# A decoder layer in float32: the second layer's v turned by VectorE and gathered through memory, or by TensorE head by head

## The chip, the cores and the metric

The kernel runs on one core of one Trainium2 chip. The metric is device time in microseconds, the median of several executions. A core has five engines that run side by side, each in the order of its own instructions: TensorE (PE in the profile, PEld for its weight loads), VectorE (DVE), ScalarE (ACT), GpSimd (POOL) and SyncE (SP), which here issues all DMAs. TensorE writes to PSUM, a small memory in banks; DMAs move data between HBM and SBUF.

## The reference, cut to what matters

Three layers follow each other, each with a residual and a layer norm. x has 16 sequences of 256 tokens with 512 channels.

```
x = layernorm(x + mamba_like(x, ...))            # first layer: projections, a causal
                                                 # convolution, a scan, gates
x = layernorm(x + xattn(x, k, bias, ctx, ctx))   # second layer
x = layernorm(x + ffn(x, ...))                   # third: W x + b, and the two best of 8 LoRA experts

# second layer, 32 heads of 8 tokens each; L = 512 channels
kv = v[b,h,i,:] * ctx[b,h,j,:]                   # outer product over i, j = 8 x 8
y  = causal_convolution(kv, k[h], along the 512) + kv * bias[h,i]
out[b,h,j,:] = sum over i of y[b,h,i,j,:] * ctx[b,h,i,:]
```

v is the output of the first layer. Its convolution along the channels is a product with a Toeplitz matrix, so v is wanted with channels on partitions, while the first layer delivers it with tokens on partitions.

## The kernel before

The program is written with a manual schedule: each engine runs its instructions in the order in which the code issues them, and only semaphores for data hold them back.

**First half** (to about 750 us). Eight groups of 512 tokens, four tiles `xs[t]` of 128 tokens x 512 channels each. The loop over `order` has ten steps `i`, each a pair of projections. At the end of a group the output products are added onto `xs`, and `normalised` (L542 to L549) takes the statistics (`layer_norm_stats`: DVE, then a power on POOL), scales the tile on DVE (L547) and stores it to the DRAM tensors `first[0]` and `first[1]` (L549, rows of 2 KB): tiles 0 and 2 at the end of the group, tiles 1 and 3 (`late`) in steps 0 and 1 of the next. Step 1 also issues the loads of the next group's x. The last group does all four tiles in the order 0, 2, 1, 3; between them it loads head 0's v.

**Second half.** A loop over the heads `h`, 0 to 31. For each, `load_v` (L140) fetches 128 rows (16 sequences x 8 tokens) of 512 channels, and `turned_v` (L147, L149) turns them with four transposes of TensorE into the PSUM tile `tr`, which ACT copies to the SBUF tile `vT`. DVE's `products` (L157) multiply `tr` with the context `cT` into `kv`; POOL adds `vT` as the residual. The rows are turned at the turn of the heads, one head before they are used.

The convolution of a head goes in two halves `q`, each into two PSUM tiles `y0` and `y1` of two banks, which exist once. So the order around the turn of a head is: the last convolution (q = 1, quadrant matmuls L1046) ends; DVE multiplies `y1`, then `y0` with `cT` (`multiplied`, L1079) and reduces them (L1089); meanwhile TensorE does `turned_v`, the transpose of the gates (`turned_gates`: L1244, ACT's copy L1246), a share of the feed-forward; then `seeded` (L1013) writes the first product of the new head to a bank of `y1`, ACT copies it to the other bank of `y1` (`spread_seed`, L1020), TensorE does another share of the feed-forward, and `convolve` goes on with its full products (L1031): the first to `y0`, the second to a bank of `y1`.

The feed-forward of two heads is one `Pair` of seven half products. From head 4 on, an even head finds the pair `opened` (its products `sixth` and `second` are due), an odd head from 5 on finds it `closing` (`seventh` and `lora_of_second`). The two lines that follow the seed in `spread_seed` are

```
for a, b in ((0, HP), (HP, 0)):
    nc.scalar.copy(bank_of(y, 2)[b : b + HP], seed[a : a + HP])
```

SP's queue in a head is: the Toeplitz tile of the next head (`load_T`, which waits for the convolution to be through), v and context of the head after next, and outputs of 256 KB.

Of the kernel before, what the change touches and what calls it, by code (L numbers as in the profile page):

```python
# [8 lines left out]
F32 = mybir.dt.float32  # L9
# [5 lines left out]
P = 128  # L15
# [15 lines left out]
NL = D // P  # L31
NE, R = 8, 16
HP = P // 2

# [36 lines left out]
def decoder_kernel(  # L73
# [34 lines left out]

    dram = ctx.enter_context(tc.tile_pool(name="dram", bufs=1, space=bass.MemoryType.DRAM))
    SH = S // P  # L110
    first = [dram.tile([B, P, D], F32, name=f"first{i}") for i in range(SH)]
    wp = ctx.enter_context(tc.tile_pool(name="w", bufs=1))

    big = ctx.enter_context(tc.tile_pool(name="big", bufs=2))
# [19 lines left out]
        nc.sync.dma_start(cT, ctxT[h])  # L134
        return cT

    def load_v(h):
        vn = q3.tile([P, D], F32, tag="vn", name="vn", bufs=1)
        sh, hs = divmod(h, P // NH)
        nc.sync.dma_start(vn, first[sh][:, hs * NH : (hs + 1) * NH, :])  # L140
        return vn

    def turned_v(vn, pool, tag):

        tr = pool.tile([P, NQ, NL, BQ * NH], F32, tag=tag, name="tr")
        for k, blk in enumerate(BLOCKS_IN):
            nc.tensor.transpose(tr[:, :, k, :], vn[:, blk * P : (blk + 1) * P], ident)  # L147
        vT = q2.tile([P, NQ, NL, BQ * NH], F32, tag="vT", name="vT")
        kept = nc.scalar.copy(vT, tr)  # L149
        return vT, tr, kept  # L150

    def products(vT, cT, kv, q, ks=(0, NL // 2), kept=None):

        full = [P, NL * BQ // 2, NH, NH]
        for k in ks:
            blks = slice(k, k + NL // 2)
            last = nc.vector.tensor_tensor(  # L157
                kv[:, q, k * BQ : (k + NL // 2) * BQ],
                vT[:, q, blks].rearrange("p k (b i) -> p (k b) i", i=NH).unsqueeze(2)
                .to_broadcast(full),  # L160
                cT[:, q, 1 + k : 1 + k + NL // 2].rearrange("p k (b j) -> p (k b) j", j=NH).unsqueeze(3)
                .to_broadcast(full),
                ALU.mult,
            )
            if kept is not None:
                wait_for(last, kept)
        return last

    def wait_for(ins, other):
# [12 lines left out]
    with ExitStack() as s1:  # L182
# [357 lines left out]
                part = w[:, kc, 0:cols]  # L540
                nc.vector.tensor_tensor(part, part, ps[:, 0:cols], ALU.subtract)

        def normalised(g, *ts):

            stats = [layer_norm_stats(nc, p2, nhalf, r, "a") for _, r in ts]
            for (t, r), (mv, rs) in zip(ts, stats):
                nc.vector.tensor_scalar(r, r, mv[:, 0:1], rs, ALU.subtract, ALU.mult)  # L547
                bi, sh = divmod(g * TT + t, SH)
                nc.sync.dma_start(first[sh][bi], r)  # L549

        heads = {}
        late, sums = [], []
        for g in range(groups):
            xs = xs_next
            more = g + 1 < groups
# [95 lines left out]
            for i, (kind, p) in enumerate(order):  # L651
# [71 lines left out]
                        w_sums = w_o_sums(behind)  # L723
                        next(w_sums)
                before = (kind, p, al, be, u, to)
                if i < 2 and late:
                    normalised(g - 1, late.pop(0))
                if i == 1 and more:
                    xs_next = load_x(g + 1)

            def spread_heads(cc):
# [94 lines left out]
            if more:  # L826
# [23 lines left out]
                for n, (al, be) in enumerate(banks):  # L850
                    out_product(al[:, 0:S], n, (0, 1), (1, 0), upon=True)
                    if n == 0:
                        next(parts)
                    out_product(be[:, 0:S], n, "S4", (1, 1), upon=True)
                    if n == 0:
                        next(parts)
                    out_product(be[:, S:], n, (1, 1), "T4", upon=True)
                    out_end_sums(n, al, be, us[n])
                    if n == 0:
                        next(parts)  # L860
                        next(parts)
                        normalised(g, (0, xs[0]), (2, xs[2]))
                late = [(1, xs[1]), (3, xs[3])]
            else:
                finish_sums()
                gated(1, spread_heads(1))
                for n, t in enumerate((0, 2, 1, 3)):


                    ps = ps_s.tile([P, 512], F32, tag="s", name="s") if n in (0, 3) else bank()  # L870
                    for c in range(NI):
                        for j in range(2):
                            nc.tensor.matmul(  # L873
                                ps[:, j * S : (j + 1) * S],
                                zs[c][:, t * P : (t + 1) * P],
                                w_o[c // HC, j][c % HC],
                                start=(c == 0 and j == 0),
                                stop=(c == NI - 1),
                                skip_group_check=True,
                            )  # L880
                        if n == 3 and c == 3:
                            heads["vT"] = turned_v(heads["vn"].pop(0), ps_t, "tr")
                            heads["vn"] = [load_v(1)]
                    if n == 3:
                        for q in range(NQ):
                            products(heads["vT"][0], cTs[0], kvs[0][0], q)
                    r = xs[t]
                    nc.vector.scalar_tensor_tensor(r, r, 2.0, ps, ALU.mult, ALU.add)
                    normalised(g, (t, r))
                    if n == 1:  # L890
                        heads["vn"] = [load_v(0)]
                        kvs = [load_T(0), load_T(1)]
            if g == 0:
                skip_bc = wp.tile([P, S], F32, name="skip_bc")
                nc.sync.dma_start(skip_bc, skip.partition_broadcast(P))
# [21 lines left out]
    with ExitStack() as s2:  # L917
# [267 lines left out]

        w_lb = w2.tile([ER, D], F32, name="w_lb")
        nc.sync.dma_start(w_lb, loraB)
        vT_next, vns = heads["vT"][0], heads["vn"]
        more_next = prepared(*kvs[0])
        sk_next = skip_sums(0, kvs[0][0])  # L1190
        more_next[2](1)
# [1 line left out]
        vT_ahead = []  # L1193

        def ahead():
            vT_ahead.append(turned_v(vns.pop(0), ps_t, "tr"))
            vns.append(load_v(2))
            cTs.append(load_c(2))

        def squares(o_l):  # L1200
# [72 lines left out]
                )[n - 1]  # L1273
                nc.gpsimd.tensor_tensor(Tw[:, n - 1], one, other, ALU.subtract)

        def half_product(ps, a, w, start=False):
            for kc in range(2):
                nc.tensor.matmul(  # L1278
                    ps, a[:, kc, :], w[:, kc, :], start=(start and kc == 0), stop=(kc == 1),
                    skip_group_check=True,  # L1280
                )

        class Pair:
# [36 lines left out]
            def sixth(self):  # L1320
                half_product(self.al[:, HI], self.S[2], Tw[:, 1])

            def second(self):
                half_product(self.al[:, LO], self.half(0, 1), corner(1, 0))

            def common(self):
                u, m = self.u, p2.tile([P, HD], F32, tag="m", name="m", bufs=1)
# [28 lines left out]
                    skip_group_check=True,  # L1356
                )

            def lora_of_second(self):
                nc.tensor.matmul(  # L1360
                    self.be[:, HI], self.xaT[1], w_lb[:, LO], start=False, stop=True,
                    skip_group_check=True,
                )
                lora(self.al, self.xaT[1], HI, True)

            def parts(self, head):
                if head == 0:
# [3 lines left out]
            def finish(self, head):  # L1371
                return Finish(self.f + head, self.parts(head), self.rs[head])

        last, xa = None, None
        pair, closing, ready = None, None, []
        for h in range(HX):
            nxt, ff, f = h + 1 < HX, last is not None, h - 1
# [7 lines left out]
            y = new_y()  # L1385
            if h:
                if nxt:
                    v_after = turned_v(vns.pop(0), ps_t, "tr")
                    kvs.append(load_T(h + 1))
                    if h + 2 < HX:  # L1390
                        vns.append(load_v(h + 2))
                        cTs.append(load_c(h + 2))
                if xa is not None:
                    xaT = turned_gates(xa, gl[:, XAT])
                    if h == 2:
                        xaT_alone = xaT
                    else:
                        pair.xaT.append(xaT)
                opened = pair if pair is not None and len(pair.o) == 2 else None
                if h == 2:  # L1400
                    feed_forward(base, alone, (1,))
                if h == 3:
                    lora(base, xaT_alone, ALL)
                if opened is not None:
                    opened.sixth()
                if closing is not None:
                    closing.seventh()
                seed = seeded(y, T, xs, 0, h == 1)
                spread_seed(y, seed, h == 1)
                if h == 2:  # L1410
                    feed_forward(base, alone, (2,))
                if opened is not None:
                    opened.second()
                if closing is not None:
                    closing.lora_of_second()
            if h < 2:
                weight_differences((3, 1) if h == 0 else (2, 4))
            if ff:
# [40 lines left out]
            behind = None  # L1459
            if nxt:  # L1460
                kv_n, T_n = kvs[0]
                cT_n, (vT_next, v_n, kept) = cTs[0], v_after
                if h:
                    behind = products(v_n, cT_n, kv_n, 0, kept=kept)

            if h:
                contract(y, cT, red, 0, (1, 0))
            else:

                prs = []  # L1470
                products(v_n, cT_n, kv_n, 0, (0,), kept)
                prs = [multiplied(y, cT, 0, i) for i in (1, 0)]
                behind = products(v_n, cT_n, kv_n, 0, (NL // 2,), kept)
                for i, pr in zip((1, 0), prs):
                    reduced(pr, red, 0, i)
            y = new_y()
# [223 lines left out]
```

## Time and profile before

| | |
|---|---|
| median of 3 runs | 1408.8 us (1408.38 to 1408.83) |
| the profiled execution | 1408.37 us, its span 1406.6 us |
| TensorE busy, weight loads | 1391.9 us, 946.6 us |
| VectorE busy | 1182.1 us |
| ScalarE, GpSimd busy | 427.5 us, 613.3 us |
| DMA, HBM read and written | 63 GB/s over the span, 70.62 and 17.32 MB |

The span goes from the first to the last instruction; the execution's time has some 1.8 us around it. The rows of a timeline are: start, duration, engine, line of the code, operation, tiles written and read, shapes, number of instructions merged, and in brackets how long the engine stood before it and what released it. A float32 matmul is recorded as two passes. "PEld" rows are weight loads; one that waits for a semaphore holds back its matmul.

### The profile page before, as it was taken

Reading aid. Unit: us, or ns where it says so; the run is one execution under the profiler, and the core shown is the slowest. Engines: PE = TensorE matmul, PEld = TensorE weight load, DVE = VectorE, ACT = ScalarE, POOL = GpSimd, SP = SyncE. Lnnn points to the kernel's source line nnn. Section 1 sums busy time; section 2 is a strip of 40 time slices with the busy share of each in tenths; the row PEclk is TensorE's granted clock in tenths of the full one; section 3 lists DMA queues with packets and bytes.
Section 4 is the critical chain, followed back from the end, with each engine's and each line's share of the span. In section 5 each row is a group of like instructions: output and inputs, shape, how many; then the busy total and the mean of one; then the engine's idle time right before and its main releaser. Section 6 shows DMA issues by size and latency. Waiting matters only on the chain.

```text
span 1406.6 us, 19577 instructions
## 1 busy us (share of the span) xinstructions
PE 1391.9 (99%) x7091; PEld 946.6 (67%) x7091; DVE 1182.1 (84%) x2269; ACT 427.5 (30%) x948; POOL 613.3 (44%) x818
## 2 busy tenths in 40 slices
PE   9999999999999999999999999999999999999997
PEld 7888888788888888878885445455545454555444
DVE  6988878878888787877867888989898898989886
ACT  2423323233232333332311223333332333333222
POOL 5450011110100201001004667887777877887774
PEclk9999999999999999999999999999999999999999
DMA  8114121120121111202103122211222122212100
GB/s 305 33 38 134 27 67 46 38 85 8 40 83 46 47 45 39 85 10 70 66 8 104 43 68 75 76 56 65 61 75 69 52 75 76 75 46 75 61 27 38
DMA packets 49169, 89.21 MB, mean 63 GB/s; under 512 B 8880, under 2 KB 13360, under 8 KB 49072
## 3 DMA queue, kind: packets, MB, share of 16 engines
q1 hardware_dynamic: 49072, 87.96, 19.7%
q8 instruction: 56, 0.92, 0.3%
q14 instruction: 41, 0.34, 0.1%
HBM read 70.62 MB, written 17.32 MB: 63 GB/s over the span
## 4 chain that ended last, share of the span: by engine, by line
PE 96%; DVE 2%; issue 1%; DMA 0%; POOL 0%; ACT 0%; SPq 0%; POOLq 0%; DVEq 0%
PE mm L330 21%; PE y L1031 15%; PE s L330 14%; PE y L1046 12%; PE s L782 6%; PE mm L782 6%; PE y L1013 4%; PE be L1278 4%; PE al L1278 3%; PE gl L1223 2%; PE tr L147 1%; PE xm L599 1%; PE mm L739 1%; PE mm L873 1%; PE al L1250 1%; PE s L873 1%
## 5 line engine op out<-in xcount | busy, mean ns | idle before, releaser
L1079 DVE TENSOR_TENSOR pr<-y,cT 128x1024 f32<-128x1024 f32 x126 | 148.5, 1220 | 50.2 <-PE y L1046 50.2
L1046 PE MATMUL y<-kv 64*64 64x512 f32 x1536 | 179.6, 598 | 0.0
L588 DVE SCALAR_TENSOR_TENSOR acc<-xi,wc,acc 128x512 f32<-128x512 f32 x192 | 141.9, 753 | 7.4 <-ACT acc L584 1.8
L1089 DVE TENSOR_REDUCE red<-pr 128x128 f32<-128x1024 f32 x126 | 147.1, 1210 | 0.0
L157 DVE TENSOR_TENSOR kv<-tr,cT 128x1024 f32<-128x1024 f32 x124 | 145.6, 1216 | 0.0
L1046 PEld LDWEIGHTS y<-kv 64*64 64x64 f32 x1536 | 52.2, 132 | 118.6 <-issue 97.1
L1031 PE MATMUL y<-kv 128*128 128x512 f32 x272 | 128.5, 594 | 1.9 <-DVE pr L1079 1.7
L68 POOL TENSOR_TENSOR rs_a<-ve_a,nhalf 128x1 f32<-128x1 f32 x32 | 18.9, 592 | 242.3 <-DVE ve_a L66 242.3
L391 POOL TENSOR_TENSOR rstd<-ms,nhalf 128x4 f32<-128x4 f32 (+1 forms) x9 | 8.5, 949 | 251.3 <-DVE ms L389 251.3
L1031 PE MATMUL y<-kv,Td 128*128 128x512 f32 x248 | 116.5, 592 | 0.0
L330 PE MATMUL mm<-XT,w_z 128*128 128x256 f32 x384 | 90.7, 379 | 0.0
L1031 PEld LDWEIGHTS y<-kv,Td 128*128 128x128 f32 x248 | 47.1, 190 | 59.3 <-issue 59.1
L1020 ACT COPY y<-y 64x512 f32<-64x512 f32 x120 | 67.0, 558 | 59.3 <-PE y L1013 57.4
L997 POOL TENSOR_TENSOR xs<-kv 128x512 f32<-128x512 f32 x63 | 80.4, 1277 | 0.1
L1031 PEld LDWEIGHTS y<-kv 128*128 128x128 f32 x272 | 50.9, 189 | 42.8 <-ACT y L1020 17.9
L330 PEld LDWEIGHTS mm<-XT,w_z 128*128 128x128 f32 x384 | 73.0, 190 | 9.9
L1428 POOL TENSOR_TENSOR ol<-o,red 128x512 f32<-128x512 f32 x31 | 39.3, 1268 | 73.1 <-DVE red L1089 73.1
L330 PE MATMUL mm<-xnT,w_z 128*128 128x256 f32 x288 | 70.7, 382 | 0.0
L223 POOL TENSOR_TENSOR XT<-xnT 128x512 f32<-128x512 f32 x7 | 9.2, 1318 | 129.0 <-PE mm L782 129.0
L1013 PE MATMUL y<-xs,kv 128*128 128x512 f32 x120 | 62.6, 604 | 0.5 <-issue 0.2
L330 PE MATMUL s<-XT,w_xi 128*128 128x256 f32 x256 | 61.0, 380 | 0.8 <-DVE XT L226 0.5
L330 PEld LDWEIGHTS mm<-xnT,w_z 128*128 128x128 f32 x288 | 54.0, 190 | 10.1 <-issue 3.0
(333 smaller groups left out, 3058.8 us busy)
## 6 DMA issues: line engine op xcount, KB each, us to landing
cT<-in_ctxT SPq DMA_DIRECT2D x32, 384.0 KB
kv<-in_toep SPq DMA_DIRECT2D x32, 384.0 KB
xt<-in_x SPq DMA_DIRECT2D x32, 256.0 KB
spread<-both SPq DMA_DIRECT2D x32, 256.0 KB
first<-xt SPq DMA_DIRECT2D x32, 256.0 KB
vn<-first SPq DMA_DIRECT2D x32, 256.0 KB
out<-res SPq DMA_DIRECT2D x31, 256.0 KB
xnT<-in_xT SPq DMA_DIRECT2D x7, 1024.0 KB
```

Source lines behind the costliest of these rows:

```text
L157: last = nc.vector.tensor_tensor(kv[:, q, k * BQ : (k + NL // 2) * BQ], vT[:, q, blks].rearrange("p k (b i) -> p (k b) i", i=NH).unsqueeze ...
L330: nc.tensor.matmul(ps, w[:, p, a, kc, :], Xs[b][:, kc, :], start=start and kc == 0, stop=stop and kc == 1, skip_group_check=upon,)
L588: ins = nc.vector.scalar_tensor_tensor(acc, xi[:, :, k : k + S], wc[:, c, k : k + 1], acc, ALU.mult, ALU.add)
L782: nc.tensor.matmul(ps, own[a][c][:, n * P : (n + 1) * P], w_o[b][c], start=start and c == 0, stop=stop and c == HC - 1, skip_group_check=upon,
L997: return nc.gpsimd.tensor_tensor(xs[:, q], moving(kv, q, 0), moving(kv, q, 1), ALU.add)
L1013: nc.tensor.matmul(seed, T[:, SHARED_AT, :], xs[:, q], start=True, stop=True)
L1020: nc.scalar.copy(bank_of(y, 2)[b : b + HP], seed[a : a + HP])
L1031: nc.tensor.matmul(bank_of(y, lb), w, moving(kv, q, mb), start=not late and lb not in begun, stop=False, skip_group_check=True,)
L1046: return nc.tensor.matmul(bank_of(y, lb)[cols], T[rows, DIAGONAL_AT, (b - a) * HP : (b - a + 1) * HP], moving(kv, q, lb)[rows], start=star ...
L1079: nc.vector.tensor_tensor(pr.rearrange("p (k b j) i -> p k b j i", k=2, j=NH), y[i].rearrange("p k (b j i) -> p k b j i", j=NH, i=NH), cT[ ...
L1089: nc.vector.tensor_reduce(red[:, q, 2 * i : 2 * i + 2, :].rearrange("p k t -> p (k t)"), pr, AX.X, ALU.add)
L1278: nc.tensor.matmul(ps, a[:, kc, :], w[:, kc, :], start=(start and kc == 0), stop=(kc == 1), skip_group_check=True,)
```

## The change

It has four parts. In the first half, ACT scales the normalised tile, with a factor and an offset that POOL makes ready; the tile's scaling stands a step or more behind its statistics. DVE then turns it in blocks of 32 x 32 in place, and four DMAs a tile store it in pieces of 32 tokens (128 bytes) to `first`, whose layout is now channel first. The first eight tokens of each sequence also go to `rows`, unturned, for head 0, which TensorE still turns. The channels of a row are interleaved (`order_in`), so that a partition of the turned v gathers its pieces.

In the second half, `load_vT` gathers a head's v, already turned, in pieces of 8 tokens (32 bytes), two heads ahead; ACT copies it from SBUF to the PSUM tile `tr` (`kept_in`), where `products` reads it as before. And the small work around the seed is laid anew: half of `second` and half of `lora_of_second` go in front of the seed, and in an even head from 4 on the transpose of the gates goes behind it. The load of the next group's x goes from step 1 to step 3 in all groups but the first.

```
-    first = [dram.tile([B, P, D], F32, name=f"first{i}") for i in range(SH)]
+    first = [dram.tile([P // TB, P, NL, B, TB], F32, name=f"first{i}") for i in range(SH)]
+    rows = dram.tile([B, NH, D], F32, name="rows")
...
+    def load_vT(h, pool, bufs):
+        vT = pool.tile([P, NL, NQ, BQ * NH], F32, tag="vT", name="vT", bufs=bufs)
         sh, hs = divmod(h, P // NH)
-        nc.sync.dma_start(vn, first[sh][:, hs * NH : (hs + 1) * NH, :])
+        tb, part = divmod(hs, TB // NH)
+        nc.sync.dma_start(
+            vT.rearrange("p k q (b i) -> p (k q b) i", i=NH),
+            first[sh][tb].rearrange("p k b t -> p (k b) t")[:, :, part * NH : (part + 1) * NH],
+        )
+        return vT.rearrange("p k q t -> p q k t")
+
+    def kept_in(vT, pool, tag):
         tr = pool.tile([P, NQ, NL, BQ * NH], F32, tag=tag, name="tr")
-        for k, blk in enumerate(BLOCKS_IN):
-            nc.tensor.transpose(tr[:, :, k, :], vn[:, blk * P : (blk + 1) * P], ident)
-        vT = q2.tile([P, NQ, NL, BQ * NH], F32, tag="vT", name="vT")
-        kept = nc.scalar.copy(vT, tr)
-        return vT, tr, kept
+        nc.scalar.copy(tr, vT)
+        return tr
...
-        def normalised(g, *ts):
-            stats = [layer_norm_stats(nc, p2, nhalf, r, "a") for _, r in ts]
-            for (t, r), (mv, rs) in zip(ts, stats):
-                nc.vector.tensor_scalar(r, r, mv[:, 0:1], rs, ALU.subtract, ALU.mult)
-                bi, sh = divmod(g * TT + t, SH)
-                nc.sync.dma_start(first[sh][bi], r)
+        def spreads_of(r):
+            mv, rs = layer_norm_stats(nc, p2, nhalf, r, "a")
+            nb = p2.tile([P, 1], F32, tag="nb_a", name="nb_a")
+            nc.gpsimd.tensor_scalar(nb, mv[:, 0:1], rs, -1.0, ALU.mult, ALU.mult)
+            return nb, rs
+        def normalised(g, t, r, stats):
+            nb, rs = stats
+            nc.scalar.activation(r, r, AF.Identity, bias=nb, scale=rs)
+            bi, sh = divmod(g * TT + t, SH)
+            if sh == 0:
+                nc.sync.dma_start(rows[bi], r[0:NH])
+        def turned(g, t, r):
+            nc.vector.transpose(r, r)
+            bi, sh = divmod(g * TT + t, SH)
+            for tb in range(P // TB):
+                nc.sync.dma_start(
+                    first[sh][tb].rearrange("(n l) k b t -> (l k) n b t", l=TB // NL)[:, :, bi],
+                    r[tb * TB : (tb + 1) * TB].rearrange("l (n t) -> l n t", t=TB),
+                )
...
-                if i < 2 and late:
-                    normalised(g - 1, late.pop(0))
-                if i == 1 and more:
+                if g:
+                    for one in turning[:2]:
+                        turned(g - 1, *one)
+                    del turning[:2]
+                    if i < 2:
+                        t, r, *_ = late[i]
+                        late[i] = t, r, spreads_of(r)
+                    if i in (1, 2):
+                        normalised(g - 1, *late[i - 1])
+                        turning.append(late[i - 1][:2])
+                if i == (3 if g else 1) and more:
                     xs_next = load_x(g + 1)
...
                     if n == 1:
-                        heads["vn"] = [load_v(0)]
+                        heads["vn"] = load_rows()
                         kvs = [load_T(0), load_T(1)]
+                        for n_, t_ in enumerate((0, 2)):
+                            turned(g, t_, xs[t_])
+                        heads["next"] = load_vT(1, q2, 2)
+                turned(g, 1, xs[1])
+                turned(g, 3, xs[3])
...
         def ahead():
-            vT_ahead.append(turned_v(vns.pop(0), ps_t, "tr"))
-            vns.append(load_v(2))
+            vT_ahead.append(kept_in(vTs[0], ps_t, "tr"))
+            vTs.append(load_vT(2, p2, 3))
             cTs.append(load_c(2))
...
                 if nxt:
-                    v_after = turned_v(vns.pop(0), ps_t, "tr")
+                    v_after = kept_in(vTs[0], ps_t, "tr")
                     kvs.append(load_T(h + 1))
                     if h + 2 < HX:
-                        vns.append(load_v(h + 2))
+                        vTs.append(load_vT(h + 2, p2, 3))
                         cTs.append(load_c(h + 2))
...
+                if opened is None:
+                    turn_gates()
...
                 if opened is not None:
                     opened.sixth()
+                    opened.second((0,))
                 if closing is not None:
                     closing.seventh()
+                    closing.lora_of_second((0,))
                 seed = seeded(y, T, xs, 0, h == 1)
+                if opened is not None:
+                    turn_gates()
                 spread_seed(y, seed, h == 1)
...
                 if opened is not None:
-                    opened.second()
+                    opened.second((1,))
                 if closing is not None:
-                    closing.lora_of_second()
+                    closing.lora_of_second((1,))
```

## The prediction

> **What bounds the kernel now.** I read the page first, then the group of line 147 (the transposes to be removed), then the timeline of single heads, engine by engine, then the DMA view. The page's engine row, its chain and its DMA queue:
>
> ```profile
> PE 1391.9 (99%) x7091; PEld 946.6 (67%) x7091; DVE 1182.1 (84%) x2269; ACT 427.5 (30%) x948; POOL 613.3 (44%) x818
> PE 96%; DVE 2%; issue 1%; DMA 0%; POOL 0%; ACT 0%; SPq 0%; POOLq 0%; DVEq 0%
> q1 hardware_dynamic: 49072, 87.96, 19.7%
> ```
>
> TensorE carries the chain, and DMA is a fifth full. The removed work, from the view of line 147:
>
> ```profile
> L147 PE MATMUL tr<-ident,vn x128: 272/273/330, 749.5 to 1344.9; 128*128 128x128 f32 x128
> ```
>
> Now the turn of one head (an even one), in the timelines of PE, PEld, DVE and ACT:
>
> ```profile
> 907.20 0.66 PE L147 MATMUL tr<-ident,vn 128*128 128x128 f32 x4
> 907.69 0.27 PE L1244 MATMUL gl<-ident,xa 128*128 128x128 f32 x1
> 907.80 1.03 PE L1278 MATMUL al<-Tw,S 128*128 128x256 f32 x4
> 908.66 1.06 PE L1013 MATMUL y<-xs,kv 128*128 128x512 f32 x2
> 909.56 1.03 PE L1278 MATMUL al<-w_f,ol 128*128 128x256 f32 x4
> 910.42 1.45 PE L1031 MATMUL y<-kv 128*128 128x512 f32 x3
> ...
> 908.59 0.30 PEld L1013 LDWEIGHTS y<-xs,kv 128*128 128x128 f32 x2 [0.17 <-issue]
> 910.96 0.51 PEld L1031 LDWEIGHTS y<-kv 128*128 128x128 f32 x2 [0.34 <-ACT y L1020]
> ...
> 907.30 2.36 DVE L1079 TENSOR_TENSOR pr<-y,cT 128x1024 f32<-128x1024 f32 x2 [1.34 <-PE y L1046]
> ...
> 909.76 1.15 ACT L1020 COPY y<-y 64x512 f32<-64x512 f32 x2 [1.06 <-PE y L1013]
> ```
>
> Call 907.20, when the last head's convolution is through, C. The reader is to see two waits that the transposes only just cover. First, the seed matmul (L1013) writes a bank that the first DVE multiplication (L1079, 1.22 us each) must have read: that ends at C+1.33, and the seed's weights load at C+1.40, held back 0.17. Second, ACT copies the seed to another bank from C+2.56 to C+3.71, and the convolution's second full product, which writes those banks, loads its weights at C+3.76, held by that copy. Its matmul starts at 910.42+2x0.43 = C+4.08. So after the second wait TensorE has only about 0.2 us in hand.
>
> **The change part by part.**
>
> *Transposes off TensorE (gain, mostly not kept).* Between the starts of 907.20 and 907.69 four transposes take 0.49 us. They stand at the turn of heads 1 to 30, 30x0.49 = 14.7 us, and once more inside head 0, where DVE is late anyway (TensorE waits 1.0 and 0.7 us for L1079 there). The Trainium skill, "TensorE: Matmul & The Clock Gate", Part 4, has about 275 ns for one transpose in a kernel; that would make 33 us. The trace has the same 273 ns as duration, but the starts lie 0.11 apart, since they are pipelined: I use 0.49 a head. Taken out, TensorE reaches the seed earlier, and the first wait stops it: DVE still ends at C+1.33, weights at C+1.40. The change puts in front of the seed 1.29 us of work in an even head (four matmuls of 0.86, two of 0.43) and 1.40 in an odd one (0.11+0.86+0.43): TensorE idles there where it transposed. Behind the seed 0.43 us of work went forward, so the gain can only appear there, and the second wait allows C+3.76 plus some 0.11 for the loading weights (what the seed shows: its two passes stand 0.47 instead of 0.43 apart): C+3.87 for C+4.08, 0.21 a head. Odd heads 5 to 31 have it: 14x0.21 = 2.9 us.
>
> *The gates' transpose moved (loss).* In even heads from 4 on, the transpose of the gates and ACT's copy of it (L1246, 0.27 us) now stand between the seed and ACT's two copies. ACT is in order: the transpose starts at 909.56, ends 0.27 later, so ACT's copies start at 910.04 to 910.17 instead of 909.76 (a copy's next neighbour starts between 0.17 and 0.30 later). That is 0.28 to 0.41 late against 0.21 in hand: 0.07 to 0.20 lost, 14 heads, 1.0 to 2.8 us; I take 1.9. Behind ACT wait the second full product and all of the convolution. Heads 0 to 3 are bound by DVE or ACT in the same places: 0.
>
> *Copy kept.* ACT's copy of v (586 ns, L149) stays, now from SBUF to PSUM, and no longer waits for TensorE: it runs in ACT's idle time before C (ACT idles 2.14 us before it now). DVE reads the same PSUM tile, six microseconds later. 0; if v were late, ACT would stand with the seed's copies queued behind it, and each microsecond would be one of the kernel.
>
> *Gather.* A head's v came as 128 rows of 2 KB; it now comes as 8192 pieces of 32 bytes. Two rows bound the price of a piece. The window of the store of `row` (512 pieces of 4 bytes) has 528 packets in 0.6 us at 41.8% of 16 engines: 7.6 ns each. The page's 49,072 packets of 1.8 KB took 19.7% of 16x1406.6: 90 ns each. A straight line gives 9 ns for 32 bytes and 13 for 128. So 512 pieces on each of 16 engines: 4.6 us; at the dear end 46 us. A rule speaks against the change: the Trainium skill, "VectorE: DVE Perf Modes", The three transpose paths, says a plain DMA that transposes by strides is 19 times slower than the crossbar, which has some 90% of DMA bandwidth. With the 390 GB/s of this trace's full stretches that is an estimate of 18.5 GB/s and 14.2 us a head. I take 4.6: the 4-byte pieces are nearer in size, and they already show scattered pieces at full pace. The gather is issued a head early, about 19 us before its copy, so either price is hidden in the steady heads: DMA is 21% busy between 850 and 1300, 4.2 us of a mean head of 19.9 (19.45 and 20.31 by turns). It stops being hidden over 15.7 us, 31 ns a piece. SP no longer waits for the transposes there; what is queued behind the gather (the context for the head after next, the output) has a head of time.
>
> *First half.* Out: 32 DVE scalings (L547, 546 ns) and the waits for POOL before them (15.9 us). In: 32 block transposes on DVE, which the trace doesn't show; 512 elements a partition are priced by L547's row, 0.55, with half and twice that as ends; on ACT 32 scalings of about 0.6 (19 us beside 427.5); on POOL 32 small ones of 0.2. Stores: 32 of 2 KB rows become 128 of 512 pieces of 128 bytes, 16 of rows, with 0.33 to 0.6 us of SP each, some 50 us of an SP that waits most of the time. A tile takes 128 pieces x13 ns = 1.7 us on each engine. SP's queue now holds stores that wait for DVE in front of the next group's x, whose load moves from the second step to the fourth; x is read at the ninth, over 30 us later. TensorE shows no stop in the half, and DVE's and ACT's added work stands where both have room. 0, with 1.5 either way; were a DVE transpose twice as dear, 18 us more on DVE, about what it loses in waits.
>
> *Turn of the halves.* Head 1's gather needs stores of the last group: x normalised on ACT at about 742.8, first the rows for head 0 (store to load took 742.46 to 744.60), two loads, then eight stores to 750.6, landed 752.7; the gather is issued at 753.3 and lands at 759.8, copied by 760.4. DVE wants it at 759.75 and now begins at 760.05: 0.4 lost. At the skill's price it lands at 769.4: about 9 lost, with head 2's behind it.
>
> Sum: -2.9 + 1.9 + 0.4 = -0.6 us. The profiled execution is 1408.4 (span 1406.6), 0.4 under the median of the three runs, 1408.8; so 1408.2.
>
> **The rivals.**
> 1. *The waits give way* (0.25). If the gates' copy fits in ACT's time, even heads gain 0.21 as well: 28x0.21 = 5.9, less 0.4, 1403.3; all 14.7 would be 1394. For it: TensorE is dense, and work was laid around the seed to fit. Against it: the weight load held at C+3.76 in every head.
> 2. *A late gather at the turn* (0.20, slower). Nothing at that place has a head of lead. About 9 us at 14 us a gather: 1417. It decides from some 5 us on.
> 3. *DMA becomes the bound* (0.12, slower). At 40 ns a piece a head needs 20.5+4.2 = 24.7 of 19.9: 30x4.8 = 144, 1553. Only the packet mean of 90 ns speaks for it, and that is bytes.
> 4. *The first half slips* (0.08): ACT's scalings delay the copies that free banks, or DVE's transposes are dear: 3 to 6 us, 1413.
> That the transposes stay can be excluded but for head 0, which keeps its four.
>
> **How the numbers follow.** The forecast has 0.35: within 3 us of 1408.2, where 0.2% is 2.8 us, about what a measurement of this kernel can tell: 0.25 same, 0.05 on either side. Faster: 0.05 and rival 1, 0.30. Same: 0.25, and 0.03 of rivals 2 and 4. Slower: 0.05, and the rest of rivals 2, 3 and 4, 0.42. Range: the forecast's own is 1405.5 to 1411; down to 1399 to take in the likelier part of rival 1, up to 1419 for rivals 2 and 4; rival 3 and a full gain stay out.
>
> **What would show it.** C to the second full product 3.87 in odd heads and 4.15 to 4.28 in even ones (4.08 both before); PE idle before the seed; the copies of L1020 behind L1246 in even heads. Packets of 32 bytes near 9 ns and DMA near 40% in the second half would bear out the gather; a queue full throughout, or DVE waiting for a copy of v, would show it wrong. If the heads shrink by 0.4 or more, my two waits were not the limit.

## The result, and the profile after

The changed kernel takes 1432.19 us, median of four runs (1430.54 to 1433.51), against 1408.59 us before (four runs, 1408.14 to 1408.83). The ratio is 1.0167, with an interval of 1.0150 to 1.0185: slower by 23.6 us, and outside the range forecast. The profiled execution took 1430.54 us with a span of 1428.4 us, 21.8 us more than the span of before. The page of after, in the same rows as those shown of before (busy times by engine, the chain by engine, the DMA queue):

```profile
PE 1393.4 (98%) x6967; PEld 930.1 (65%) x6967; DVE 1183.3 (83%) x2269; ACT 448.1 (31%) x980; POOL 619.9 (43%) x850
PE 81%; DVE 9%; DMA 3%; ACT 2%; issue 1%; SPq 1%; POOL 1%; POOLq 0%; DVEq 0%
q1 hardware_dynamic: 362288, 88.23, 33.4%
```

TensorE has 124 instructions fewer, so 31 heads did lose their four transposes. Yet its share of the chain fell from 96% to 81%: DVE, DMA and ACT now hold 14% of it (before: 2%). DVE's busy time grew by 1.2 us and ACT's by 20.6, and ACT is busy for 31% of the span alone, so the time went into waits.

Where it went shows when one compares the starts of the same instruction in the two traces. The table gives how much later (in us, from the start of each span) an instruction of after and of each experiment starts than that of before. "Head n" is the first of its 64-row matmuls; the seed of head 0 stands about 8 us behind them in before.

```
kernel                   head 0     seed of head 0  head 1   head 4   head 31   end
after                    +15.77         +22.01      +22.01   +22.20   +21.63   +21.84
e1_own_tile               -0.33          +5.86       +5.86    +6.05    +5.48    +5.74
e2_last_on_dve           +14.72         +14.33      +21.18   +21.36   +20.77   +21.18
e3_old_small_work        +18.14         +24.70      +24.70   +24.70   +24.70   +24.72
e4_pieces_of_16          +15.26         +20.50      +22.83   +23.01   +22.44   +22.66
e5_gates_first            -0.17          +5.10       +5.10    +4.88    -0.95    -0.75
e6_turn_and_heads         +0.41          +0.02       +0.85    +0.64    -5.18    -4.97
e7_stores_only            -0.20          +5.11       +5.11    +5.29    +4.67    +4.90
```

So of the 21.8 us, 15.8 are lost before head 0 begins, 6.2 within head 0 (in after all of them ahead of its seed), and the heads from 1 on together give back 0.2. (The loss of the first half differs between runs: in the four profiled kernels that have the in-place turn it is 14.7 to 18.1 us.)

**In the first half.** Two rows of the view of waits (engine and line that waited, what for: us in total, times, longest); neither has a counterpart before:

```profile
DVE xt L578 <- DMA rows<-xt: 39.3, 8, 6.0
...
PE mm L348 <- DVE u L378: 11.7, 9, 2.1
```

Behind seven of the eight waits of the first row TensorE falls back by 1.3 to 2.8 us each, 15.1 us in all. The eighth stands in the last group, and there nothing more is lost before head 0. One such place in the timeline of all engines (start, duration, engine and line, operation; in brackets how long the engine stood and for what):

```profile
202.37 0.81 ACT L571 ACTIVATE xt<-xt,nb_a,rs_a 128x512 f32<-128x512 f32 x1 [0.28 <-POOL nb_a L565]
202.50 1.84 SPq L492 DMA_DIRECT2D spread<-both  x3
...
204.44 0.76 SPq L574 DMA_DIRECT2D rows<-xt  x2
...
210.09 1.30 DVE L578 STREAM_TRANSPOSE xt<-xt 128x512 f32<-128x512 f32 x2 [5.21 <-DMA rows<-xt]
...
220.88 1.47 PE L348 MATMUL mm<-xnT,w_xi 128*128 128x256 f32 x5 [1.62 <-DVE u L378]
```

Read it from the top. ACT has scaled the tiles at 203.2. Their first eight rows are stored to `rows`, which SP issues at 204.44, behind three loads of `spread`. DVE turns the tile in place, so it may not write before that store has read the tile: it stands 5.21 us, until 210.09. Everything in DVE's queue is now late, among it `u` (L378, at 220.41), which reads a PSUM bank that TensorE needs again: TensorE stands 1.62 us for it before 220.88. The DMA reads only eight rows, but the DVE instruction overwrites all 128.

**At the turn of the halves.** The timelines of ACT, PE and DVE inside head 0, and below them ACT's row of before for the same copy `one`:

```profile
774.03 0.81 ACT L571 ACTIVATE xt<-xt,nb_a,rs_a 128x512 f32<-128x512 f32 x1 [7.54 <-POOL nb_a L565]
774.75 0.17 ACT L1112 COPY one<-nhalf 128x1 f32<-128x1 f32 x1
...
774.98 1.99 PE L1096 MATMUL y<-kv 64*64 64x512 f32 x8 [3.78 <-ACT one L1112]
...
776.90 7.15 PE L1081 MATMUL y<-kv 128*128 128x512 f32 x12
...
783.22 2.36 DVE L1129 TENSOR_TENSOR pr<-y,cT 128x1024 f32<-128x1024 f32 x2 [5.92 <-PE y L1081]
```

```profile
754.64 0.19 ACT L1062 COPY one<-nhalf 128x1 f32<-128x1 f32 x1 [3.92 <-PE y L1046]
```

The scaling of the last tile, which DVE did before, now stands in ACT's queue and waits 7.54 us for the tile's statistics by way of POOL. (In the last group the code issues a tile's scaling right behind its statistics, not a step later as in the other groups.) Behind it stands `one` (L1112), the small copy that the last eight passes of head 0's 64-row matmuls need; before the change it ran at 754.64, 1.15 us after head 0 began. TensorE stands 3.78 us. And the products after it are slow: 7.15 us for twelve passes that take 5.32 us before and 5.42 us in the experiments that remove the stand. The windows tell why (length; busy time and count of PE, PEld, DVE, ACT and POOL; then the granted clock, the DMA share and GB/s):

```profile
770.00:775.00 5.00, 1.22 (x15) 0.17 (x8) 3.51 (x8) 0.89 (x2) 1.81 (x3) 0.86 1.08 64
775.00:780.00 5.00, 5.00 (x12) 1.79 (x13) 2.30 (x3) 0.59 (x1) 4.84 (x6) 0.50 0.79 127
```

After the idle stretch the granted clock is 0.50; in the next 5 us it is 0.96 again.

**In the steady heads** the two steps of the forecast are to be seen. An even head, with C = 929.15, and an odd one, with C = 948.78, in the timelines of PE and PEld:

```profile
929.15 1.13 PE L1328 MATMUL al<-Tw,S 128*128 128x256 f32 x4
...
933.32 1.13 PE L1081 MATMUL y<-kv 128*128 128x512 f32 x2 [0.24 <-ACT y L1070]
934.28 0.59 PE L1081 MATMUL y<-kv,Td 128*128 128x512 f32 x1
```

```profile
948.78 0.33 PE L1294 MATMUL gl<-ident,xa 128*128 128x128 f32 x1
...
951.58 2.10 PE L1081 MATMUL y<-kv 128*128 128x512 f32 x4
952.55 0.30 PEld L1081 LDWEIGHTS y<-kv 128*128 128x128 f32 x2 [0.78 <-ACT y L1070]
...
953.51 1.45 PE L1081 MATMUL y<-kv,Td 128*128 128x512 f32 x3
```

The second full product of the even head starts at 933.32, C+4.17. In the odd head it is the last two of the four passes of 951.58; their weights load at 952.55, C+3.77. In both heads, with the weights loaded only then, the second pass follows 0.53 to 0.54 us after the first, where passes otherwise stand 0.43 apart. What comes behind is therefore as late as if the product had started at C+4.27 and C+3.87 (two passes of 0.43 us before 934.28 and 953.51, where the next product starts). Before, both were at C+4.08.

### The profile page after: what moved, and what is told of

Its sections match the earlier page's. It is cut to its first block, busy times and chain, and to the rows that moved or that the text cites. A ratio compares the mean times of both kernels' runs of the same rounds, so it can differ in the third digit from the quotient of the medians.

```text
span 1428.4 us, 19590 instructions
## 1 busy us (share of the span) xinstructions
PE 1393.4 (98%) x6967; PEld 930.1 (65%) x6967; DVE 1183.3 (83%) x2269; ACT 448.1 (31%) x980; POOL 619.9 (43%) x850
## 4 chain that ended last, share of the span: by engine, by line
PE 81%; DVE 9%; DMA 3%; ACT 2%; issue 1%; SPq 1%; POOL 1%; POOLq 0%; DVEq 0%
PE mm L348 16%; PE y L1081 15%; PE y L1096 11%; PE s L348 9%; PE s L825 6%; PE mm L825 4%; PE y L1063 4%; PE be L1328 3%; DMA rows<-xt 2%; PE al L1328 2%; DVE acc L623 2%; PE gl L1273 2%; ACT y L1070 1%; PE xm L634 1%; PE mm L782 1%
## 5 line engine op out<-in xcount | busy, mean ns | idle before, releaser
L177 DVE TENSOR_TENSOR kv<-tr,cT 128x1024 f32<-128x1024 f32 x128 | 150.2, 1216 | 2.7 <-ACT vT L152 2.7
L1081 PE MATMUL y<-kv 128*128 128x512 f32 x272 | 137.1, 612 | 5.6 <-ACT y L1070 3.3
L1487 POOL TENSOR_TENSOR ol<-o,red 128x512 f32<-128x512 f32 x31 | 39.3, 1269 | 70.2 <-DVE red L1139 70.2
```

The costliest lines, as they stand in the source:

```text
L177: last = nc.vector.tensor_tensor(kv[:, q, k * BQ : (k + NL // 2) * BQ], vT[:, q, blks].rearrange("p k (b i) -> p (k b) i", i=NH).unsqueeze ...
L1081: nc.tensor.matmul(bank_of(y, lb), w, moving(kv, q, mb), start=not late and lb not in begun, stop=False, skip_group_check=True,)
```

## The experiments

My theory after the result was that the loss has two places, and neither is in the heads. (1) The in-place turn makes DVE wait for the store of rows. (2) At the turn of the halves the work of the last tile holds up head 0. The rivals: the small pieces of the gather crowd the DMA queues and so slow the stores and loads; or the new order of the small work in the heads is what costs.

**e1_own_tile: the turned tile gets memory of its own where the rows are stored as well.** Only DVE's wait for the store goes; all transfers stay.

```
 def turned(g, t, r):
-    nc.vector.transpose(r, r)
     bi, sh = divmod(g * TT + t, SH)
+    own = r
+    if sh == 0:
+        own = p2.tile([P, D], F32, tag="acc", name="turned", bufs=6)
+    nc.vector.transpose(own, r)
+    r = own
```

> Edit to the changed kernel: the block transpose of tiles 0 and 2 writes to a tile of its own instead of in place, so it need not wait until the store of the first eight rows has read the tile (39.3 us of DVE waits in 8 places). Theory 1, that wait delays the first half: head 0's convolution, which stands 15.8 us later than before, comes back by 12 to 16 us, and the time falls from 1432 to 1416 to 1420. Rival, ACT's scaling in front of the copies that free banks, or the small stores and x's later load on SP: the time stays within 3 us of 1432, and DVE's wait is replaced by another in the same place.

Measured: 1413.97 us (1413.34 to 1414.81), ratio to before 1.0037 (1.0022 to 1.0051). Head 0 begins 0.33 us earlier than before the change, instead of 15.77 later. The timeline of SP and DVE at the same place as above:

```profile
201.49 0.76 SPq L574 DMA_DIRECT2D rows<-xt  x2
201.84 1.30 DVE L582 STREAM_TRANSPOSE turned<-xt 128x512 f32<-128x512 f32 x2
```

DVE turns the tiles 0.35 us after the store was issued, without a wait. Theory 1 holds, and for more than I had expected of it: the whole loss of the first half was this one wait. All else in that half (32 transposes on DVE, 32 scalings on ACT, 128 stores of 128-byte pieces) costs nothing there. What is left, 5.7 us of the span, comes from the turn, which still loses 6.2.

**e2_last_on_dve: the last tile of the last group is scaled by DVE, as before**, so that `one` has no such wait in front of it on ACT.

```
-        def normalised(g, t, r, stats):
+        def normalised(g, t, r, stats, on_dve=False):
             nb, rs = stats
-            nc.scalar.activation(r, r, AF.Identity, bias=nb, scale=rs)
+            if on_dve:
+                nc.vector.tensor_scalar(r, r, nb, rs, ALU.subtract, ALU.mult)
+            else:
+                nc.scalar.activation(r, r, AF.Identity, bias=nb, scale=rs)
...
-                    normalised(g, t, r, spreads_of(r))
+                    if n == 3:
+                        mv, rs = layer_norm_stats(nc, p2, nhalf, r, "a")
+                        normalised(g, t, r, (mv[:, 0:1], rs), True)
+                    else:
+                        normalised(g, t, r, spreads_of(r))
```

> Edit to the changed kernel: the very last tile of the first half is scaled by DVE, as before the change, and not by ACT. Theory 1, the turn of the halves loses 6.2 us because ACT's small copy in head 0's convolution stands behind that scaling, which waits for statistics, and TensorE idles 3.8 us and then gets half its clock for some 5 us: the time falls by 4 to 6.5 us to about 1427. Rival, the gather for head 1 lands late and holds ACT or DVE there: no more than 1 us is won, and ACT's copy of v waits for a DMA.

Measured: 1431.91 us (1429.94 to 1432.02), ratio 1.0160 (1.0145 to 1.0176). A miss: the wait goes, the time stays. The timelines of ACT, PE and DVE:

```profile
769.36 0.19 ACT L1119 COPY one<-nhalf 128x1 f32<-128x1 f32 x1 [3.92 <-PE y L1103]
...
770.94 5.42 PE L1088 MATMUL y<-kv 128*128 128x512 f32 x12
774.82 0.59 ACT L169 COPY tr<-vT 128x512 f32<-128x512 f32 x1 [5.26 <-DMA vT<-first]
...
780.73 2.36 DVE L1136 TENSOR_TENSOR pr<-y,cT 128x1024 f32<-128x1024 f32 x2 [3.51 <-DMA first<-xt]
...
783.14 3.78 PE L1088 MATMUL y<-kv 128*128 128x512 f32 x4 [5.92 <-DVE pr L1136]
```

`one` is early again, TensorE goes through at full clock (5.42 us), and the seed of head 0 has lost nothing more since head 0 began (14.33 against 14.72). Then a second wait comes to light that had lain under the first: DVE's first product waits 3.51 us for the stores of the last tiles. `pr` reads nothing of them, so I take this for a wait for memory: its tile would lie where a tile of the ended half is still being stored. Before, those stores were single DMAs of whole rows; now they are eight for the two tiles, issued after the turning. TensorE stands 5.92 us behind `pr`, and its granted clock from 780 to 785 us is 0.53, so this wait, too, costs more than itself. From this comes theory 2: there are two waits, and either of them alone costs the time. Note also the third row: ACT waits 5.26 us for the gather of head 1, and nobody waits behind it.

**e3_old_small_work: all of the small work behind the seed and the gates in front of it, as before the change; only the transposes are gone.**

```
-                if opened is None:
-                    turn_gates()
+                turn_gates()
...
-                    opened.second((0,))
...
-                    closing.lora_of_second((0,))
...
-                if opened is not None:
-                    turn_gates()
...
-                    opened.second((1,))
+                    opened.second()
...
-                    closing.lora_of_second((1,))
+                    closing.lora_of_second()
```

> Edit to the changed kernel: the small work around the seed is laid as before the change (second and lora_of_second whole behind the seed, the gates' transpose in front in all heads); only TensorE's transposes stay away. Theory 1, two waits (DVE's first product, then ACT's copies) fix the turn of a head: with 0.43 us more behind the seed the second full product stands 4.08 us after the convolution's end in even and odd heads, as before the change, so heads are as long as before although TensorE has 0.49 us less to do in each: even 19.45, odd 20.31, and the whole within 1 us of the changed kernel. Rival, TensorE's work is the bound: every head is 0.3 to 0.5 us shorter than before the change, the whole 9 to 15 us less than the changed kernel.

Measured: 1433.3 us in one run. The heads answer the question by themselves: in the table the distance to before is 24.70 us from head 1 to head 31. The mean periods are 20.311 us for the even heads and 19.449 for the odd ones, against 20.312 and 19.448 before. (Here and below a period is named after the head at whose turn it is spent; the expectation above counts each from the head's own start, so there the two are exchanged.) So the transposes, alone, gave TensorE nothing at all: 0.49 us of its work is out in each head and every head takes as long. The timeline of PEld in an even head, with C = 931.90, has both waits of the prediction at their places:

```profile
933.30 0.30 PEld L1063 LDWEIGHTS y<-xs,kv 128*128 128x128 f32 x2 [0.61 <-POOL xs L1047]
...
935.66 0.51 PEld L1081 LDWEIGHTS y<-kv 128*128 128x128 f32 x2 [0.34 <-ACT y L1070]
```

C+1.40 and C+3.76, to the hundredth what they were with the transposes. (The profile names POOL's `xs` for the first. That ended at 932.81. DVE's two products started at 932.00 and take 1.22 us each, so the first ended at about 933.2; the start fits DVE.)

**e4_pieces_of_16: the gather in two DMAs with pieces half as long**, 16,384 of 16 bytes a head: the DMA price doubled, against the rival of crowded queues.

```
-        nc.sync.dma_start(
-            vT.rearrange("p k q (b i) -> p (k q b) i", i=NH),
-            first[sh][tb].rearrange("p k b t -> p (k b) t")[:, :, part * NH : (part + 1) * NH],
-        )
+        for a in (0, NH // 2):
+            nc.sync.dma_start(
+                vT.rearrange("p k q (b i) -> p (k q b) i", i=NH)[:, :, a : a + NH // 2],
+                first[sh][tb].rearrange("p k b t -> p (k b) t")[
+                    :, :, part * NH + a : part * NH + a + NH // 2
+                ],
+            )
```

> Edit to the changed kernel: each gather is cut in two DMAs of 8192 pieces of 16 bytes, so twice the pieces for the same bytes. Theory 1, the gather is hidden with room to spare: the DMA share between heads 5 and 25 rises from about 0.5 to 0.65 or more, head lengths stay within 0.05 us, the time changes by less than 3 us, and only the turn of the halves may lose up to 5. Rival, DMA is close to being the bound: heads grow by 1 us or more, 30 us in all.

Measured: 1431.48 us (1427.92 to 1433.00), ratio 1.0157 (1.0142 to 1.0172): no slower than the change. The window of 866 to 1275 us, of before, after and this kernel in this order:

```profile
866.00:1275.00 409.00, 409.00 (x2067) 207.44 (x2060) 368.88 (x622) 130.30 (x317) 323.62 (x427) 1.00 0.21 68
```

```profile
866.00:1275.00 409.00, 406.62 (x1985) 196.62 (x1987) 370.52 (x637) 131.96 (x321) 326.88 (x434) 1.00 0.49 67
```

```profile
866.00:1275.00 409.00, 406.62 (x1979) 196.75 (x1981) 370.46 (x637) 131.32 (x319) 327.77 (x432) 1.00 0.80 66
```

The DMA share went from 0.21 to 0.49 with the change and to 0.80 here, at the same bytes, and the heads keep their periods (20.501 us for even and 19.232 for odd ones after, 20.498 and 19.235 here). The gather is hidden, with room for twice its pieces. Only at the turn does the dearer gather show: from head 0 to head 1 this kernel loses 7.6 us (22.83 less 15.26), 2.3 of them behind the seed of head 0, where after loses nothing. The rival falls.

**e5_gates_first: e1, and the transpose of the gates in front of the seed in all heads.**

```
-                if opened is None:
-                    turn_gates()
+                turn_gates()
...
                 seed = seeded(y, T, xs, 0, h == 1)
-                if opened is not None:
-                    turn_gates()
```

> The run with the tile of its own, and in it the gates' transpose stands in front of the seed in even heads too, as odd heads have it. Theory 1: in even heads ACT's two copies of the seed are no longer held back, so the second full product goes from 4.27 to 3.87 us after the convolution's end, an even head loses 0.41 us as against the run before (14 heads, 5.7 us): even period 20.09, odd 19.23, time 1408.3. Rival, DVE has no room for shorter even heads: they stay at 20.3 or more and the time at 1411 to 1414.

Measured: 1407.71 us (13 runs, 1407.32 to 1409.14) against 1408.97, ratio 0.9994 (0.9985 to 1.0002): not told apart from before. The periods are 20.096 us for even and 19.232 for odd heads: both are now 0.22 us shorter than before. From head 4 to head 31 the kernel gains 5.8 us (table: +4.88 to -0.95), which pays for the 5.3 us that the turn still costs.

**e7_stores_only and e6_turn_and_heads: the two waits of the turn, one by one and together.** e7 is e1 with the stores of the last group mended: tile 1 is turned and stored a step earlier, and all four tiles are turned into memory of their own. ACT still scales the last tile.

```
-            if sh == 0:
+            if sh == 0 or g == groups - 1:
...
-                turned(g, 1, xs[1])
+                    if n == 2:
+                        turned(g, 1, xs[1])
                 turned(g, 3, xs[3])
```

> The run with the tile of its own, and only the stores' part of the turn taken away (tile 1 turned earlier, tiles of their own in the last group); ACT still scales the last tile. Theory 2, two waits lie over each other: taking away one alone wins nothing, TensorE still idles 3.8 us for ACT's small copy and loses its clock, 1413.5 to 1414.5. Rival, the stores alone were the turn's cost: 1408 to 1410.

Measured: 1413.37 us (1413.16 to 1414.70), ratio 1.0032 (1.0021 to 1.0044), against 1.0037 of e1, and 0.1 us below the range expected. From head 0 to its seed it still loses 5.3 us, as e5 does without the edit of the stores. PE's and DVE's timelines:

```profile
759.01 1.09 PE L1101 MATMUL y<-kv 64*64 64x512 f32 x8 [3.78 <-ACT one L1117]
760.02 7.12 PE L1086 MATMUL y<-kv 128*128 128x512 f32 x12
...
766.32 2.36 DVE L1134 TENSOR_TENSOR pr<-y,cT 128x1024 f32<-128x1024 f32 x2 [4.24 <-PE y L1086]
```

DVE's first product waits for TensorE and not for a store, and the wait for `one` and the slow products stand as in after. As e2 took away the one wait and gained nothing, e7 takes away the other and gains nothing. e6 takes away both: it is e5 with the edits of e2 and e7.

> As gates_first, and at the turn of the halves three things: the last tile is scaled by DVE, tile 1 is turned and stored a step earlier, and in the last group all tiles are turned to tiles of their own, so that the stores do not hold memory that DVE's first product of the second half writes. Theory 2 (formed on the run last_on_dve, where ACT's wait went and a wait of DVE for stores of 3.5 us came in its place): both waits together make the turn's 6.2 us, and without both it falls to 0 to 1.5 us: time 1402.5 to 1404. Rival, the gather for head 1 is what comes next: DVE or ACT waits for it and the turn keeps 3 us or more, 1405 to 1408.

Measured: 1403.46 us (five runs, 1403.07 to 1404.84), ratio to before 0.9962 (0.9948 to 0.9975). It is the fastest version: 5.5 us faster than the kernel before the change and 28.7 faster than the change. Its timelines of ACT, PE and DVE in head 0:

```profile
755.06 0.19 ACT L1124 COPY one<-nhalf 128x1 f32<-128x1 f32 x1 [3.92 <-PE y L1108]
...
756.64 5.42 PE L1093 MATMUL y<-kv 128*128 128x512 f32 x12
760.27 0.59 ACT L169 COPY tr<-vT 128x512 f32<-128x512 f32 x1 [5.03 <-DMA vT<-first]
762.37 2.34 DVE L1141 TENSOR_TENSOR pr<-y,cT 128x1024 f32<-128x1024 f32 x2
```

`one` is early, the products run in 5.42 us, and `pr` starts without a wait. It starts at 762.37, while packets of the last store still run until 763.86; in e2 they ended at 780.19, and `pr` started at 780.73. So `pr` needs nothing of the stores themselves: what it waited for in e2 was the memory that they held, as supposed. The turn costs 0.4 us (+0.41 at the start of head 0, +0.85 at head 1). Theory 2 is shown: two waits over each other, and only both together give the time back. (e2 lacks e1's tile, which e6 and e7 have; so the losses are counted from head 0 on.) What the earlier turning of tile 1 and the tiles of their own are each worth was not tried.

## Why the prediction was wrong

- **First half, "0, with 1.5 either way": this step failed, by 15.8 us.** I priced instructions and DMA issues, and found room for all of them; e1 shows that the room was there. What I left out is a wait that the change adds: an operation in place, behind a store that reads the same tile, waits for a transfer, here for 4.9 us on the mean of eight (39.3 us). I looked at SP's queue for what its stores would hold up in front of the next x, and not at DVE's queue for what a store holds up there. Rival 4 had the place and the sign, but put it down to ACT's scalings or dear transposes and to 3 to 6 us; e1 keeps both and loses nothing there.
- **Turn of the halves, "0.4 lost": this step failed, by 5.8 us.** I followed the gather of head 1 and nothing else. The gather was as I had it: issued at 768.12 and copied at 774.82 in e2, 6.7 us where I had 6.5 to landing. In e6, with the same gather, the whole turn costs 0.4 us, but that this is the number forecast is chance: nobody waits for the gather there, and DVE has the transpose of the last tile (0.71 us) in front of `pr`. What I did not follow is the scaling moved from DVE to ACT: behind it in ACT's queue stands `one`, on which TensorE waits. Nor did I ask whose memory the eight late stores keep from coming free. Rival 2 named this place, and a mechanism that was not the cause. Rival 4's mechanism, a copy held up by a scaling on ACT, is near to the first of the two waits, but it was set in the first half.
- **Transposes off TensorE, "mostly not kept": right.** e3 has the gain of the transposes alone at 0.00 us a head. In odd heads the second full product counts as starting at C+3.87, as forecast (with the first pass at C+3.77 and the slower step to the second); their period fell by 0.216 us for 0.21.
- **The gates' transpose moved, 0.07 to 0.20 lost in even heads: right, at the upper end.** Counted in the same way, C+4.27 lies in the 4.15 to 4.28 forecast; the period grew by 0.189 us. Together the heads gave back 0.6 us from head 4 to head 31 (1.0 forecast). e5 takes the step away, and both kinds of head gain 0.22: the 5.8 us that its heads gain are near rival 1's sum of 5.9, but come by another order, in which the gates' copy stands ahead of ACT's copies of the seed.
- **Gather: hidden, as forecast; the skill's rule did not apply.** The packets of the trace: 254,080 of 32 bytes with a median of 9 ns, and 65,664 of 128 bytes with 13 ns, both as the straight line gave. The mean of the small ones is 11 ns, so the DMA share of the window is 0.49 where about 0.40 was forecast. The 14.2 us, my estimate from the Trainium skill, "VectorE: DVE Perf Modes", The three transpose paths, did not come: 6.7 us from issue to copy. The page ties its factor of 19 to a large stride of the innermost dimension at the destination, and here DVE has turned the tile beforehand, so that the 8 tokens of a piece lie side by side at both ends. I should have left the rule out of the estimate.
- **Copy kept, 0: right in the steady heads.** The only waits of ACT for a gather in e6 are two at the turn, 5.9 us in all, with nobody held up by them.
- **Small durations**: the DVE transpose took 0.70 us (0.55 taken), ACT's scaling 0.81 (0.6). Without weight, since e1's first half is no longer than that of before.

The range was drawn around costs of operations; these waits were not among its cases.

## What to carry to other kernels

Before an operation is moved onto another engine's queue or made in place, list for each of its tiles who still reads it, and how long that reader takes to let go: a store that reads eight rows held the in-place turn for 5 us, and a tile of its own gave all of the 15.8 us back. Where an engine is in order, the first thing to look for behind a moved instruction is the small one that another engine waits for, above all at the turn between two stages. And when the removal of one wait gains nothing, look in the trace for the next one at the same place before giving up the theory: here neither of two gained alone, and without both the turn costs 0.4 us instead of 6.2.

## What the hardware showed that I had not expected

A short idle stretch costs more than itself. TensorE stood 3.78 us, and then had a granted clock of 0.50 in the next 5 us: twelve passes took 7.15 us for 5.42, 1.7 us more. The length of the slow stretch is not fixed. At the turn the clock stood at 0.50 for 6.8 us in after, e1, e2 and e3, and for 3.4 us in e4, e5 and e7. The stand of 3.78 us, which all of these but e2 have, cost 6.2 to 6.6 us from head 0 to its seed where the slow stretch was the longer one, and 5.2 to 5.3 where it was the shorter. So it came to 1.5 to 2.8 us more than the stand, and the length of the slow stretch accounts for e5 and e7 losing less there than e1. What decides between the two lengths no run here shows.

The Trainium skill, "TensorE: Matmul & The Clock Gate", has in the section "Why this matters for your kernels" that idle gaps above about 3 us between matmuls bring the clock down to half. The stands of 3.78 us agree with it, and so does e6, whose longest stand in head 0 is 1.86 us and whose clock stays at 1.00. But 3 us is not a safe limit: in e3 a shorter stand in the first half was enough (PE's timeline, then a window with the fields as above):

```profile
127.39 3.16 PE L348 MATMUL mm<-xnT,w_xi 128*128 128x256 f32 x8 [2.57 <-DVE u L378]
```

```profile
128.10:131.40 3.30, 3.30 (x9) 2.52 (x9) 2.16 (x6) 2.21 (x5) 0.00 (x0) 0.50 0.23 35
```

After a stand of 2.57 us the clock is 0.50, and the eight passes take 3.16 us. In e4 TensorE stands 2.57 us at the same place as well, but the clock stays at 1.00, and the eight passes take 2.11 us. Against before, e3 loses 5.2 us at this one place and e4 3.1, and this difference is most of the 2.9 us by which e3 is behind e4 at head 0 (18.14 and 15.26 in the table). A new wait of some 3 us of an otherwise dense TensorE must be priced with it.

DMA pieces far below a row's length went through at 9 ns each (the median) on each engine, at 32 bytes and at 16: halving them raised the DMA share from 0.49 to 0.80 at the same bytes, without any cost in the heads.
